# Loads of replicated tiles: four requests of 32 rows each, or one request of 128 rows, in a convolution-plus-scan kernel on one core

## The chip, the core and the metric

The kernel runs on one NeuronCore of one Trainium2 chip. The metric is the device time of one execution in microseconds (us). Three runs of the kernel before took 9806.04, 9808.63 and 9807.86 us; the median is 9807.86 us.

## What is computed

The input is 8 images of 256 channels and 48 x 48 = 2304 positions ("tokens"), float32. There are two layers, and each adds its result to its input after a group normalization (32 groups of 8 channels).

Layer 0 compares every token with every other and averages the features of the 16 nearest:

```python
feat_pos = tokens @ W.T + bias            # 256 features, 256 position channels
pos = pos / max(norm(pos), 1e-12)
sim = einsum('bnc,bmc->bnm', pos, pos)    # 2304 x 2304 per image
topksim, topkid = top_k(sim, 16)
out = einsum('bnk,bnkc->bnc', softmax(topksim), feat[topkid])
```

Layer 1 is a selective scan, two blocks deep (DEPTH = 2). With 512 inner channels (d) and 16 states (s) it is, for each token t in order,

```python
dA = exp(dt_t[:, :, None] * A)                                  # A is (512, 16)
h  = h * dA + dt_t[:, :, None] * B_t[:, None, :] * x_t[:, :, None]
y  = einsum('bds,bs->bd', h, C_t)
```

with a layer norm, an input projection, a causal convolution of 4 taps, SiLU and softplus before it, and a gate and an output projection behind it.

## The kernel before

**Units and steps.** Layer 1 is cut into chunks of T = 384 tokens, so 6 chunks for each of 8 images and 2 blocks: 96 units. A unit has 16 steps (STEPS = 512 / G with G = 32 channels) and each step has two parts, so a unit has 32 parts (HOOKS). In a step the 128 partitions hold 32 channels times J = 4 groups of states, and each partition carries Q = 4 states of 384 tokens. The step therefore needs its 32 rows of step sizes (`dt`) and of dt times x (`dtx`) four times, once in each quarter of the partitions, and the unit needs each row of B and of C in the 32 partitions of its group. These replicated tiles are `dtr`, `dtxr` and `BC`. They are made by writing `dt`, `dtx` and B, C to HBM (`times_x` L798, `split` L771) and reading them back (`load_rep` L615, `load_bc` L628). Each of the three kinds has three buffers.

**A step on the engines.** GpSimd (POOL) multiplies B by dtx (`make_bx`, L853), two steps ahead. ScalarE (ACT) makes the decays exp(dt A) into PSUM, two for each part (`decay`, L877). VectorE (DVE) runs the scan of a part, 770 elements (`run_scan`, L892). The product with C is then made by one of two engines: the strings SHARE say for each part of a unit whether POOL ("G", `pool_part`, L920) or DVE ("V", L894) does it. A step with "GG" is one POOL instruction of 1536 elements, a step with one "G" is one of 768. SHARE has three strings: the first for the nine units of an image that have the top-k beside them, the second for the other three, the third for the last image. TensorE (PE) sums the states (`sum_states`, L938).

**Order.** The order on each engine is the order in which the program names the instructions. The loop over parts at the end calls `carry`, `decay`, `make_bx`, `pool_part`, then the entries of a timetable for this part that stand before the scan (`between`), the scan, and the entries behind it (`behind`). An entry such as `(-8, load_rep, "dtx", 0)` puts that call 8 parts before its unit's first. Units with no top-k beside them use `between_spare` and `behind_spare`. All loads and stores of this phase are DMA requests in the queue of SyncE (SP), in that order; a request that waits for a semaphore holds what is behind it in this queue.

**Layer 0 beside it.** The first image's layer 0 runs alone; that of image n+1 runs beside the scan of image n (`Ahead.go`), with a table of its own (`within`) for each block of 128 tokens. `finish` (L535) adds a block's result, transposed in PSUM, to x, with the features' bias, and takes statistics for the next group normalization. `group_stats` (L187) combines them to a scale and a shift per channel.

**PSUM.** There are 8 banks. In the scan phase two decay tiles take 4, the tag "mm" takes 3 for all other products, and "po", the average of a block (`weigh`, L508), has one. When layer 0 runs alone, "mm" has 5 and "po" 2.

Of the kernel before, what the change touches and what calls it, by code (L numbers as in the profile page):

```python
# [15 lines left out]
P = 128  # L16
# [9 lines left out]
def tile_conv_preact(  # L26
# [45 lines left out]


    SHARE = (
        "GGVGGGVVGGGGGGVGGGVVGGGVGGGGGGVG",
        "GGGGVGVVGVVVGVGVGGGGVGVGGVVVGVGV",
        "VGVGVGVGVGVGGGVGGGVVVGVVGGVVGGVG",
    )
    assert N % T == 0 and N % P == 0 and T % P == 0 and NS % (J * HQ) == 0

# [106 lines left out]
    def group_stats(st, found, mm0, name):  # L187
# [69 lines left out]

    def layer0(b, left, pool, ps0, alone):
        def mm0(w, name):
            return ps0.tile([P, 512], F32, tag="mm", name=name, bufs=5 if alone else 3)[:, :w]  # L260

        more = 2 if alone else 1
        depth = 2 if alone else 1
# [271 lines left out]
        def finish(t):  # L535
            row = blocks[t]
            xr = row["xr"]

            for cb in range(CB):
                nc.vector.scalar_tensor_tensor(  # L540
                    xr[:, cb, :], row["pr"][:, cb * P : (cb + 1) * P], b_feat[:, cb : cb + 1],
                    xr[:, cb, :], ALU.add, ALU.add,
                )
                nc.vector.bn_stats(st1[:, cb, t, :], xr[:, cb, :])
            nc.sync.dma_start(x1[:, t * P : (t + 1) * P].rearrange("(k p) t -> p k t", p=P), xr)
            row.clear()
# [22 lines left out]
                f(t, *args)  # L569
            yield  # L570
        found = []
        yield from group_stats(st1, found, mm0, f"b{b}")
        left.update(x1=x1, rstd=found[0], shift=found[1])

    lefts = [{} for _ in range(B)]
# [29 lines left out]
        return banks[m % 2][:, 511 - T : 513 + T]  # L605

    def mm(w, name):
        return ps.tile([P, 512], F32, tag="mm", name=name, bufs=3)[:, :w]

# [5 lines left out]
    def load_rep(unit, what, ik):  # L615
# [345 lines left out]
    def leave(unit, cb):  # L961
# [22 lines left out]
        (10, load_rep, "dtx", 9), (21, load_rep, "dtx", 14), (11, gate, 0), (-29, spread_root),  # L984
        (0, times_x, 3), (-19, load_in, 5), (33, load_out), (8, load_rep, "dtx", 8), (-22, load_in, 0),
        (21, load_rep, "dt", 13), (-20, tap, 0), (-10, step_size, 1), (9, copy_z, 2), (-18, in_proj, 2),
        (2, load_rep, "dtx", 5), (10, sum_states, 0), (13, load_rep, "dt", 9), (29, gate, 2), (9, silu_z),
        (7, load_rep, "dt", 6), (19, load_rep, "dt", 12), (-6, load_rep, "dtx", 1), (-14, load_in, 7),
        (-30, root), (9, load_rep, "dt", 7), (4, load_d, 1), (-24, load_in, 3), (17, load_rep, "dt", 11),
        (14, load_rep, "dtx", 11), (-13, x_proj), (-17, load_in, 6), (-3, load_d, 0), (4, load_rep, "dtx", 6),  # L990
        (-4, load_rep, "dtx", 2), (-42, load_v),
    ]
    behind = [
        (-12, split), (-3, load_rep, "dt", 1), (3, in_proj, 4), (-10, step_size, 0), (-3, load_rep, "dt", 0),
        (-8, load_rep, "dtx", 0), (-15, tap, 3), (-1, load_rep, "dt", 2), (-28, scale),
        (16, load_rep, "dtx", 12), (11, load_rep, "dt", 8), (8, in_proj, 6), (17, sum_states, 1),
        (-14, silu_x), (25, load_rep, "dt", 15), (-37, affine), (1, times_x, 2), (7, copy_z, 0),
        (10, load_rep, "dtx", 10), (-17, tap, 2), (-10, softplus), (-16, in_proj, 3), (3, load_rep, "dt", 4),
        (-29, load_in, 2), (6, in_proj, 7), (35, gate, 3), (-2, load_rep, "dtx", 3), (8, copy_z, 1),
        (40, leave, 1), (22, load_rep, "dtx", 15), (-8, load_in, 4), (29, load_d, 3), (-37, mean),  # L1000
        (-19, taps, 0), (-19, in_proj, 1), (-10, load_bc, 0), (33, sum_states, 3), (-30, root_end),
        (-9, times_x, 0), (-20, load_in, 1),
    ]
    between_spare = [
        (-34, center), (24, sum_states, 2), (-34, variance), (-21, in_proj, 0), (38, out_proj, 0),
        (-15, taps, 2), (-14, taps, 3), (-35, square), (39, leave, 0), (20, load_rep, "dt", 14),
        (5, load_rep, "dt", 5), (-4, load_bc, 1), (38, out_proj, 1), (17, load_d, 2), (-17, tap, 1),
        (18, load_rep, "dtx", 13), (-8, times_x, 1), (19, gate, 1), (-22, normal), (9, load_rep, "dtx", 8),
        (1, load_rep, "dt", 3), (0, load_rep, "dtx", 4), (14, load_rep, "dt", 10), (6, load_rep, "dtx", 7),
        (10, load_rep, "dtx", 9), (-18, taps, 0), (12, load_rep, "dtx", 10), (20, load_rep, "dtx", 14),  # L1010
        (11, gate, 0), (-1, times_x, 2), (-22, spread_root), (-19, load_in, 5), (33, load_out),
        (-22, load_in, 0), (21, load_rep, "dt", 13), (-20, tap, 0), (-10, step_size, 1), (9, copy_z, 2),
        (-18, in_proj, 2), (2, load_rep, "dtx", 5), (10, sum_states, 0), (13, load_rep, "dt", 9),
        (29, gate, 2), (9, silu_z), (7, load_rep, "dt", 6), (19, load_rep, "dt", 12), (-6, load_rep, "dtx", 1),
        (-14, load_in, 7), (37, gate, 3), (-31, root), (9, load_rep, "dt", 7), (5, load_d, 1),
        (-24, load_in, 3), (17, load_rep, "dt", 11), (14, load_rep, "dtx", 11), (-13, x_proj),
        (-17, load_in, 6), (-3, load_d, 0), (4, load_rep, "dtx", 6), (-4, load_rep, "dtx", 2), (-42, load_v),
    ]
# [114 lines left out]
```

## Time and profile before

| | us |
|---|---|
| median of three runs | 9807.86 |
| the profiled execution | 9813.77 |
| its span, first to last instruction | 9812.0 |
| VectorE busy | 8904.6 (91%) |
| GpSimd busy | 9023.9 (92%) |
| TensorE busy | 7958.7 (81%) |
| ScalarE busy | 7304.4 (74%) |
| DMA queue of SP, share of 16 engines | 47.7% |

The profiled execution took 1.8 us more than its span. All durations of instructions below are from it. Busy times are averages over a span whose first 450 us, layer 0 of the first image, look different from the rest; so the shares are to be read by stage. The page's DMA lists give requests by what they write and read ("dtxr<-dtx_d"), their number, the size of one and the median time from issue to landing. The DMA share is the mean over 16 DMA engines: a share of 0.49 says nothing on how evenly the work lies on them.

### The profile page before, as it was taken

To read this page: it belongs to the slowest core of one execution; us is meant where nothing else is said; L and a number is where in the kernel's file an instruction comes from. 1 tells how busy PE (TensorE), PEld (TensorE's weight loads), DVE (VectorE), ACT (ScalarE), POOL (GpSimd) and SP (SyncE) were. 2 spreads that over 40 slices of the span, in tenths; PEclk is the share of its full clock that TensorE was granted. 3 is DMA by queue.
4 is the path that set the end of the run, shared out by engine and by line. 5 is a ranking of instruction groups with operands and counts; after the bars stand their busy time and mean duration, and the time that the engine had idled before them with its cause. 6 is when DMAs were issued, how large, how long until landed. Compare 5 with 4: busy or idle time off the path is not lost.

```text
span 9812.0 us, 133959 instructions
## 1 busy us (share of the span) xinstructions
PE 7958.7 (81%) x36761; PEld 4336.7 (44%) x36761; DVE 8904.6 (91%) x7864; ACT 7304.4 (74%) x15938; POOL 9023.9 (92%) x3971
## 2 busy tenths in 40 slices
PE   8888887888878887788877888778887788866665
PEld 6644443444434444444434445344443444422222
DVE  5599998999989999899988999899998999989898
ACT  4577877777777777777777787777786778767776
POOL 1199998999989999899999999999998999999999
PEclk9989998999989998899988999889998999977777
DMA  1244455545454445444454445544545454545554
GB/s 35 58 124 132 126 139 139 135 123 140 127 147 126 134 131 144 132 129 132 132 144 131 132 129 135 141 134 124 137 130 150 121 137 125 140 134 138 144 142 122
DMA packets 1241872, 1269.02 MB, mean 129 GB/s; under 512 B 266496, under 2 KB 1214208, under 8 KB 1241120
## 3 DMA queue, kind: packets, MB, share of 16 engines
q1 hardware_dynamic: 1240576, 1260.46, 47.7%
q8 instruction: 293, 4.80, 0.2%
q14 instruction: 459, 3.76, 0.1%
q10 hardware_dynamic: 544, 0.00, 0.0%
HBM read 1046.58 MB, written 212.86 MB: 128 GB/s over the span
## 4 chain that ended last, share of the span: by engine, by line
DVE 33%; ACT 24%; DMA 11%; PE 11%; SPq 10%; issue 7%; POOL 4%; ACTq 0%; DVEq 0%; POOLq 0%
DVE bx L892 11%; ACT da L877 10%; SPq L625 8%; DVE da L892 8%; DVE xc L751 5%; DMA dtr<-dt_d 4%; DVE bx L894 3%; DMA BC<-bc_d 3%; DVE top L464 2%; DVE left L467 2%; POOL bx L920 2%; PE po L514 2%; POOL bx L853 2%; DMA dtxr<-dtx_d 2%; ACT rest L486 1%
## 5 line engine op out<-in xcount | busy, mean ns | idle before, releaser
L853 POOL TENSOR_TENSOR bx<-BC,dtxr 128x1536 f32<-128x1536 f32 x1536 | 5296.3, 3454 | 144.5 <-PE y L938 72.8
L877 ACT ACTIVATE da<-dtr,A_sb 128x385 f32<-128x385 f32 x6144 | 3588.1, 584 | 868.6 <-DVE bx L892 375.1
L892 DVE TENSOR_TENSOR_SCAN bx<-da,bx 128x770 f32<-128x770 f32 x2073 | 3578.1, 1747 | 263.6 <-ACT da L877 232.4
L920 POOL TENSOR_TENSOR bx<-bx,BC 128x1536 f32<-128x1536 f32 (+1 forms) x1311 | 3353.6, 2558 | 70.5 <-DVE bx L892 66.0
L892 DVE TENSOR_TENSOR_SCAN da<-da,bx 128x770 f32<-128x770 f32 x999 | 1752.0, 1754 | 123.7 <-ACT da L877 81.2
L651 PE MATMUL pe<-vn,inw 128*128 128x384 f32 (+1 forms) x3072 | 1214.7, 526 | 329.6 <-issue 50.9
L514 PE MATMUL po<-feat,aT 128*128 128x256 f32 x5184 | 1352.3, 410 | 12.8 <-ACT aT L503 5.7
L938 PE MATMUL y<-bx,sel 128*32 128x384 f32 x12288 | 1266.0, 536 | 109.9 <-POOL bx L920 103.1
L443 PE MATMUL psim<-pos 128*128 128x512 f32 x2520 | 1215.2, 612 | 154.3 <-DVE xr L540 70.1
L514 PEld LDWEIGHTS po<-feat,aT 128*128 128x128 f32 x5184 | 1022.4, 203 | 343.1 <-issue 107.2
L894 DVE TENSOR_TENSOR bx<-da,BC 128x768 f32<-128x768 f32 x999 | 957.2, 958 | 34.4
L651 PEld LDWEIGHTS pe<-vn,inw 128*128 128x128 f32 x3072 | 566.9, 199 | 845.8 <-issue 206.2
L938 PEld LDWEIGHTS y<-bx,sel 128*32 128x32 f32 x12288 | 395.5, 118 | 961.5 <-issue 692.7
L443 PEld LDWEIGHTS psim<-pos 128*128 128x128 f32 x2520 | 478.0, 205 | 724.2 <-issue 375.5
L751 DVE SCALAR_TENSOR_TENSOR xc<-pe,cw,xc 128x384 f32<-128x384 f32 x1152 | 696.4, 611 | 43.4 <-ACT xc L743 16.3
L781 PE MATMUL pd<-dbl,dtp_sb 16*128 16x384 f32 x768 | 441.4, 689 | 336.5 <-ACT dt L790 189.9
L503 ACT ACTIVATE aT<-pt 128x512 f32<-128x512 f32 (+1 forms) x720 | 387.5, 548 | 419.8 <-PE pt L495 417.8
L956 PE MATMUL pw<-z,ow 128*128 128x384 f32 x1536 | 557.0, 509 | 112.8 <-ACT aT L503 52.4
L494 PE MATMUL pt<-ident,sim 128*128 128x128 f32 x2592 | 541.2, 290 | 18.5 <-ACT aT L503 13.6
L935 PE MATMUL y<-xc,dmat 128*128 128x384 f32 x768 | 398.3, 606 | 171.7 <-ACT h_st L930 58.5
L908 ACT COPY h_st<-da 128x2 f32<-128x2 f32 x808 | 128.6, 159 | 542.2 <-DVE bx L894 537.8
L495 PE MATMUL pt<-minus,rest 128*128 128x128 bf16 x2592 | 492.9, 224 | 5.9 <-ACT rest L486 5.8
(155 smaller groups left out, 9966.9 us busy)
## 6 DMA issues: line engine op xcount, KB each, us to landing
dtxr<-dtx_d SPq DMA_DIRECT2D x6144, 48.0 KB, 1.9
dtr<-dt_d SPq DMA_DIRECT2D x6144, 48.0 KB, 1.9
BC<-bc_d SPq DMA_DIRECT2D x768, 192.0 KB, 3.9
inw<-in_in_wT_dram SPq DMA_DIRECT2D x768, 128.0 KB, 2.3
dtx_d<-dtx SPq DMA_DIRECT2D x384, 192.0 KB, 2.3
dt_d<-dt SPq DMA_DIRECT2D x384, 192.0 KB, 2.3
ow<-in_out_wT_dram SPq DMA_DIRECT2D x96, 512.0 KB, 4.0
dmat<-diag SPq DMA_DIRECT2D x384, 64.0 KB, 2.2
```

The source lines that it names most:

```text
L443: nc.tensor.matmul(pm, pos[:, k, t * P : (t + 1) * P], pos[:, k, c0 : c0 + w], start=(k == 0), stop=(k == CB - 1),)
L514: nc.tensor.matmul(row["po"], aT[:, m % PT, :], feat[:, m, :], start=(m == 0), stop=(m == NB - 1))
L625: nc.sync.dma_start(rows[j * G : (j + 1) * G], src[:, i0, :])
L651: nc.tensor.matmul(pe, w[:, k], unit["vn"][:, k, lo:], start=(k == 0), stop=(k == CB - 1))
L751: nc.vector.scalar_tensor_tensor(unit["xc"][e], unit["pe"][e][:, k : k + T], cw[:, unit["d"], e, k : k + 1], unit["xc"][e], ALU.mult, ALU.add,
L853: nc.gpsimd.tensor_tensor(bx[:, :, 1:], unit["BC"][0], unit["dtxr"][i].unsqueeze(1).to_broadcast([P, Q, T]), ALU.mult,)
L877: nc.scalar.activation(da[:, s * (1 + T) : (s + 1) * (1 + T)], unit["dtr"][i], AF.Exp, scale=A_sb[:, unit["d"], i, p * HQ + s : p * HQ + s ...
L892: nc.vector.tensor_tensor_scan(h, da, g, 0.0, ALU.mult, ALU.add)
L894: nc.vector.tensor_tensor(bx[:, :, 0:T], da.rearrange("p (q t) -> p q t", q=HQ)[:, :, 1:], unit["BC"][1][:, qs], ALU.mult,)
L920: nc.gpsimd.tensor_tensor(g[:, :, 0:T], g[:, :, 1:], unit["BC"][1][:, qs], ALU.mult)
L938: nc.tensor.matmul(y[j * G : (j + 1) * G, :], sel, unit["bx"][k * J + j][:, q, 0:T], start=False, stop=True, skip_group_check=True,)
L956: nc.tensor.matmul(pw, unit["ow"][:, k, cb * P : (cb + 1) * P], unit["z"][k], start=(k == 0), stop=(k == DB - 1),)
```

## The change

There are five edits.

1. `load_rep` and `load_bc`: a tile is loaded by one request. Its source is read four times over (dt, dtx), or each of four pieces 32 times over (B, C). The number of these requests falls from 6144 + 6144 + 768 to 1536 + 1536 + 192; the bytes written are the same.
2. PSUM: the tile "po" is taken from the tag "mm", which has 4 banks beside the scan (7 when layer 0 runs alone).
3. SHARE: some parts change from POOL to DVE and the other way.
4. The features' bias: `finish` adds a block in one instruction of 256 elements, without bias. The bias is added to the group's means before they are combined (`group_stats`, `more`), enters the shift, and is added once more to the final result (`leave`).
5. The timetables: a few entries move by up to 4 parts (the loads of dt 15 and dtx 14, `affine`, `center`, `scale`, `spread_root`, `times_x` 2), and some lines stand in another order.

The core of the diff:

```diff
-        "GGVGGGVVGGGGGGVGGGVVGGGVGGGGGGVG",
-        "GGGGVGVVGVVVGVGVGGGGVGVGGVVVGVGV",
-        "VGVGVGVGVGVGGGVGGGVVVGVVGGVVGGVG",
+        "GGVGGGVVGGGGGGVGGGVVGGGVGGGGGVVG",
+        "GVGGVGVVGVVVGVGVGGGGVGVVGVGVGVGV",
+        "VGVGVGVGVGVVGGGVGGGVVGVVGVVGGGVG",
...
+        if more is not None:
+            nc.vector.tensor_add(mv[:, :, 0], mv[:, :, 0], more)
...
-        nc.gpsimd.tensor_mul(shift, mean, rstd)
-        nc.gpsimd.tensor_scalar(shift, shift, -1.0, None, ALU.mult)
+        if more is None:
+            nc.gpsimd.tensor_scalar(shift, mean, -1.0, None, ALU.mult)
+        else:
+            nc.gpsimd.tensor_sub(shift, more, mean)
+        nc.gpsimd.tensor_mul(shift, shift, rstd)
...
-            return ps0.tile([P, 512], F32, tag="mm", name=name, bufs=5 if alone else 3)[:, :w]
+            return ps0.tile([P, 512], F32, tag="mm", name=name, bufs=7 if alone else 4)[:, :w]
...
-                row["po"] = ps0.tile([P, 512], F32, tag="po", name=f"po_{b}_{t}", bufs=more)[:, :C]
+                row["po"] = mm0(C, f"po_{b}_{t}")
...
+            nc.vector.tensor_add(xr, xr, row["pr"].rearrange("p (k t) -> p k t", k=CB))
             for cb in range(CB):
-                nc.vector.scalar_tensor_tensor(
-                    xr[:, cb, :], row["pr"][:, cb * P : (cb + 1) * P], b_feat[:, cb : cb + 1],
-                    xr[:, cb, :], ALU.add, ALU.add,
-                )
                 nc.vector.bn_stats(st1[:, cb, t, :], xr[:, cb, :])
...
         src = unit[f"{what}_d"][k].rearrange("(i g) t -> g i t", g=G)
-        for j in range(J):
-            nc.sync.dma_start(rows[j * G : (j + 1) * G], src[:, i0, :])
+        nc.sync.dma_start(rows, src[:, i0, :].partition_broadcast(J))
...
-        for j in range(J):
-            r0 = i * NS + j * Q
-            nc.sync.dma_start(
-                t[j * G : (j + 1) * G].rearrange("p q t -> p (q t)"),
-                unit["bc_d"][r0 : r0 + Q, :].rearrange("q t -> (q t)").partition_broadcast(G),
-            )
+        src = unit["bc_d"][i * NS : (i + 1) * NS, :].rearrange("(j q) t -> j (q t)", j=J)
+        nc.sync.dma_start(
+            t.rearrange("p q t -> p (q t)"), src.unsqueeze(1).to_broadcast([J, G, Q * T])
+        )
...
-            nc.vector.tensor_add(res[:, cb, :], res[:, cb, :], unit["pw"][cb])
+            nc.vector.scalar_tensor_tensor(
+                res[:, cb, :], unit["pw"][cb], b_feat[:, cb : cb + 1], res[:, cb, :], ALU.add, ALU.add
+            )
```

Of the timetables, `(25, load_rep, "dt", 15)` in `behind` becomes `(28, load_rep, "dt", 15)` and `(21, load_rep, "dtx", 14)` becomes `(19, load_rep, "dtx", 14)`; in the spare tables `(20, load_rep, "dtx", 14)` becomes `(17, load_rep, "dtx", 14)`, `(-34, center)` becomes `(-36, center)`, `(-22, spread_root)` becomes `(-26, spread_root)` and `(-21, scale)` becomes `(-25, scale)`.

More of the change, by code (lines that the diff above doesn't have):

```diff
@@ L185, in rsqrt_end, with group_stats @@
         eng.scalar_tensor_tensor(r, var, 1.5, r, ALU.subtract, ALU.mult)
-    def group_stats(st, found, mm0, name):
+    def group_stats(st, found, mm0, name, more=None):
         mv = small.tile([P, CB, 2], F32, tag="gn_mv", name=f"mv_{name}")
@@ L571, in layer0 @@
         found = []
-        yield from group_stats(st1, found, mm0, f"b{b}")
+        yield from group_stats(st1, found, mm0, f"b{b}", b_feat)
         left.update(x1=x1, rstd=found[0], shift=found[1])
@@ L607, in mm @@
     def mm(w, name):
-        return ps.tile([P, 512], F32, tag="mm", name=name, bufs=3)[:, :w]
+        return ps.tile([P, 512], F32, tag="mm", name=name, bufs=4)[:, :w]
     def load_rep(unit, what, ik):
@@ L983, in tile_conv_preact @@
         (1, load_rep, "dt", 3), (0, load_rep, "dtx", 4), (15, load_rep, "dt", 10), (6, load_rep, "dtx", 7),
[L984 to L991, printed above, removed]
+        (10, load_rep, "dtx", 9), (11, gate, 0), (-29, spread_root), (0, times_x, 3), (-19, load_in, 5),
+        (33, load_out), (8, load_rep, "dtx", 8), (-22, load_in, 0), (21, load_rep, "dt", 13), (-20, tap, 0),
+        (-10, step_size, 1), (9, copy_z, 2), (-18, in_proj, 2), (2, load_rep, "dtx", 5), (10, sum_states, 0),
+        (13, load_rep, "dt", 9), (29, gate, 2), (9, silu_z), (7, load_rep, "dt", 6), (19, load_rep, "dt", 12),
+        (-6, load_rep, "dtx", 1), (-14, load_in, 7), (-30, root), (9, load_rep, "dt", 7), (4, load_d, 1),
+        (-24, load_in, 3), (17, load_rep, "dt", 11), (14, load_rep, "dtx", 11), (-13, x_proj),
+        (-17, load_in, 6), (-3, load_d, 0), (4, load_rep, "dtx", 6), (-4, load_rep, "dtx", 2), (-42, load_v),
     ]
@@ L996, in tile_conv_preact @@
         (16, load_rep, "dtx", 12), (11, load_rep, "dt", 8), (8, in_proj, 6), (17, sum_states, 1),
[L997 to L1000, printed above, removed]
@@ L1001, in tile_conv_preact @@
-        (-19, taps, 0), (-19, in_proj, 1), (-10, load_bc, 0), (33, sum_states, 3), (-30, root_end),
-        (-9, times_x, 0), (-20, load_in, 1),
+        (-14, silu_x), (28, load_rep, "dt", 15), (-39, affine), (2, times_x, 2), (7, copy_z, 0),
+        (19, load_rep, "dtx", 14), (10, load_rep, "dtx", 10), (-17, tap, 2), (-10, softplus),
+        (-16, in_proj, 3), (3, load_rep, "dt", 4), (-29, load_in, 2), (6, in_proj, 7), (35, gate, 3),
+        (-2, load_rep, "dtx", 3), (8, copy_z, 1), (40, leave, 1), (22, load_rep, "dtx", 15), (-8, load_in, 4),
@@ L1003, in tile_conv_preact @@
+        (29, load_d, 3), (-37, mean), (-19, taps, 0), (-19, in_proj, 1), (-10, load_bc, 0),
+        (33, sum_states, 3), (-30, root_end), (-9, times_x, 0), (-20, load_in, 1),
     ]
     between_spare = [
-        (-34, center), (24, sum_states, 2), (-34, variance), (-21, in_proj, 0), (38, out_proj, 0),
-        (-15, taps, 2), (-14, taps, 3), (-35, square), (39, leave, 0), (20, load_rep, "dt", 14),
-        (5, load_rep, "dt", 5), (-4, load_bc, 1), (38, out_proj, 1), (17, load_d, 2), (-17, tap, 1),
@@ L1008, in tile_conv_preact @@
[L1008 to L1016, printed above, removed]
+        (24, sum_states, 2), (-34, variance), (-21, in_proj, 0), (38, out_proj, 0), (-15, taps, 2),
@@ new lines, in tile_conv_preact @@
+        (-14, taps, 3), (-35, square), (39, leave, 0), (20, load_rep, "dt", 14), (5, load_rep, "dt", 5),
+        (-4, load_bc, 1), (38, out_proj, 1), (17, load_d, 2), (-17, tap, 1), (18, load_rep, "dtx", 13),
+        (-8, times_x, 1), (19, gate, 1), (-22, normal), (9, load_rep, "dtx", 8), (1, load_rep, "dt", 3),
+        (0, load_rep, "dtx", 4), (14, load_rep, "dt", 10), (6, load_rep, "dtx", 7), (10, load_rep, "dtx", 9),
+        (-18, taps, 0), (12, load_rep, "dtx", 10), (17, load_rep, "dtx", 14), (11, gate, 0), (-1, times_x, 2),
@@ new lines, in tile_conv_preact @@
+        (-19, load_in, 5), (33, load_out), (-22, load_in, 0), (21, load_rep, "dt", 13), (-20, tap, 0),
+        (-10, step_size, 1), (9, copy_z, 2), (-18, in_proj, 2), (2, load_rep, "dtx", 5), (10, sum_states, 0),
+        (13, load_rep, "dt", 9), (29, gate, 2), (9, silu_z), (7, load_rep, "dt", 6), (19, load_rep, "dt", 12),
+        (-6, load_rep, "dtx", 1), (-14, load_in, 7), (37, gate, 3), (-31, root), (9, load_rep, "dt", 7),
+        (5, load_d, 1), (-24, load_in, 3), (17, load_rep, "dt", 11), (14, load_rep, "dtx", 11), (-13, x_proj),
@@ L1017, in tile_conv_preact @@
         (-17, load_in, 6), (-3, load_d, 0), (4, load_rep, "dtx", 6), (-4, load_rep, "dtx", 2), (-42, load_v),
+        (-36, center), (-26, spread_root),
     ]
@@ L1020, in tile_conv_preact @@
         (-12, split), (-3, load_rep, "dt", 1), (4, in_proj, 4), (-10, step_size, 0), (-5, load_rep, "dt", 0),
-        (-8, times_x, 3), (-8, load_rep, "dtx", 0), (-15, tap, 3), (-1, load_rep, "dt", 2), (-21, scale),
+        (-8, times_x, 3), (-8, load_rep, "dtx", 0), (-15, tap, 3), (-1, load_rep, "dt", 2),
         (16, load_rep, "dtx", 12), (11, load_rep, "dt", 8), (8, in_proj, 6), (17, sum_states, 1),
@@ L1026, in tile_conv_preact @@
         (-16, load_in, 4), (29, load_d, 3), (-38, mean), (-21, in_proj, 1), (-12, load_bc, 0),
-        (33, sum_states, 3), (-31, root_end), (-9, times_x, 0), (-25, load_in, 1),
+        (33, sum_states, 3), (-31, root_end), (-9, times_x, 0), (-25, load_in, 1), (-25, scale),
     ]
```

## The prediction

> **What bounds the kernel now.** I read the busy shares and the chain first, then busy time by stage, then the costly groups by form, and last the DMA lists, because the change is mostly one of DMA requests.
>
> ```profile
> PE 7958.7 (81%) x36761; PEld 4336.7 (44%) x36761; DVE 8904.6 (91%) x7864; ACT 7304.4 (74%) x15938; POOL 9023.9 (92%) x3971
> DVE 33%; ACT 24%; DMA 11%; PE 11%; SPq 10%; issue 7%; POOL 4%; ACTq 0%; DVEq 0%; POOLq 0%
> ```
>
> ```profile
> 453.00:8424.00 7971.00, 6655.50 (x30907) 3633.03 (x30906) 7418.31 (x6530) 6113.08 (x13366) 7644.69 (x3278) 0.91 0.49 133
> 8424.00:9812.00 1388.00, 904.33 (x3760) 401.51 (x3758) 1246.95 (x1067) 970.69 (x2112) 1333.48 (x552) 0.79 0.51 136
> ```
>
> The second fence gives PE, PE's loads, DVE, ACT and POOL busy in the scan phase. POOL is at 96% in both stretches, DVE at 93% and 90%: there is at most 4% to win without lightening POOL. The chain changes hands often, and 10% of it is SP's queue issuing. The timeline gives the pace: the store of B and C, once in a unit, is issued at 438.55 (unit 0), 8725.82 (unit 84) and 9691.27 us (unit 95), so a unit takes 98.7 us with layer 0 beside it and 87.8 us in the last image.
>
> ```profile
> L853 POOL TENSOR_TENSOR bx<-BC,dtxr 128x1536 f32<-128x1536 f32 x1536 | 5296.3, 3454 | 144.5 <-PE y L938 72.8 <-DMA dtxr<-dtx_d 37.6 <-ACT da L877 23.6
> L877 ACT ACTIVATE da<-dtr,A_sb 128x385 f32<-128x385 f32 x6144 | 3588.1, 584 | 868.6 <-DVE bx L892 375.1 <-DMA dtr<-dt_d 255.3 <-DVE bx L894 94.4
> L920 POOL TENSOR_TENSOR bx<-bx,BC 128x1536 f32<-128x1536 f32 x762 | 2427.1, 3185 | 60.4 <-DVE bx L892 56.0 <-DVE den L479 1.0 <-DMA dtxr<-dtx_d 0.3
> L894 DVE TENSOR_TENSOR bx<-da,BC 128x768 f32<-128x768 f32 x999 | 957.2, 958 | 34.4
> L920 POOL TENSOR_TENSOR bx<-bx,BC 128x768 f32<-128x768 f32 x549 | 926.5, 1688 | 10.1 <-DVE bx L892 10.1
> ```
>
> The replicated loads now cost waits of 255.3 us on ACT and 37.6 us on POOL, in 9812.
>
> ```profile
> DMA packets 1241872, 1269.02 MB, mean 129 GB/s; under 512 B 266496, under 2 KB 1214208, under 8 KB 1241120
> q1 hardware_dynamic: 1240576, 1260.46, 47.7%
> ...
> dtxr<-dtx_d SPq DMA_DIRECT2D x6144, 48.0 KB, 1.9
> dtr<-dt_d SPq DMA_DIRECT2D x6144, 48.0 KB, 1.9
> BC<-bc_d SPq DMA_DIRECT2D x768, 192.0 KB, 3.9
> ```
>
> The DMA engines look half idle. That holds only if a request lies on all 16.
>
> ```profile
> 8.00:10.00 2.00, 0.00 (x0) 0.00 (x0) 1.98 (x7) 0.00 (x0) 0.00 (x0) 1.00 1.07 398
> ```
>
> This is the one full stretch (8 to 10 us, queued loads, rows of 1536 B mostly): share 1.07 at 398 GB/s, so one engine moves 24.9 GB/s.
>
> **The requests, row first.** By the trace every request runs on 16 engines: SP issues 15,918, times 16 is 254,688, and the page has 266,496 packets under 512 B, which fits one completion packet per engine and request, with some small rows. If that stays so, a tile of 4 x 49,152 = 196,608 B lands about like dt_d's store of the same size (2.3 us), its last quarter earlier than now (four issues at a median of 419 ns, 1.7 us, against one).
>
> [...]
>
> **What four engines cost.** A dt or dtx tile is 49,152 B per engine, at 24.9 GB/s 1.97 us; a B or C tile 196,608 B, 7.90 us. A unit has 32 and 2: 63.0 + 15.8 = 78.8 us. The rest: all tiles together are 3072 x 0.1966 + 192 x 0.7864 = 755 MB of 1260.46; of the other 505 some 23 lie before 453 us, so 482 / 96 = 5.0 MB a unit over 16 engines, 12.6 us on each. Sum 91.4 us of a unit's 98.7, 93%; in the last image layer 0's 0.83 MB a unit fall away, 89.4 against 87.8, 102%. So the four are just full on average, and the order decides:
> - Parts -10 to 2 of a unit (12 of 32, 37.0 us) carry both B and C (15.8), twelve dt/dtx tiles (23.6), six stores (6 x 0.49), `load_v` and small ones (1.6): 44 us, 7 behind.
> - `load_rep dtx 0` waits in SP's queue for the store of dtx 0, which stands behind B's 7.9 us on the four engines. SP issues nothing meanwhile, and they run dry for an issue and a landing, some 2.5 us.
> - The tiles have three buffers, so a load goes out at most about two steps (12.3 us) before it is needed; that hides a part of the 9.5. I take 6 us late per unit with layer 0 (0 if hidden, 12 if nothing is) and 10 in the last image.
>
> 84 x 6 + 12 x 10 = 624 us. Who waits: ACT's decays for `dtr`, then DVE's scan, and POOL's L853 for `dtxr`.
>
> SP's own issuing falls from 13,056 of these requests to 3264; at 0.42 us, 4.1 ms of queue time go. It is worth only what arrives earlier: at most the 293 us of waits above, and nothing when the engines behind are full. A request of the new form may take from 0.34 us (dtx_d's store of 128 rows) to 1.7 us (the four it replaces); either hides behind the transfer of 1.97.
>
> **SHARE.** Units by string: 63, 21, 12. G+G steps fall from 762 to 666, steps with one G rise from 549 to 657, V parts from 999 to 1083. POOL: -96 x 3.185 + 108 x 1.688 = -123 us. DVE: +84 x 0.958 = +80 us. ACT's carries (159 to 180 ns): +13 us.
>
> **Bias.** `finish`: 288 x 339 ns go. 144 additions of 256 elements from PSUM come: between 128x384 (L973, 537) and 128x768 (L685, 945) the slope is 1.06 ns an element, so 401 ns; 57.7 - 97.6 = -40 us on DVE. L973 becomes the form of L751 (611): 96 x 74 ns = +7. `more`: 8 x 161 ns (L185) = +1 us, on the path only for image 0's statistics. POOL has two small instructions either way.
>
> Sum: POOL -123, DVE +48. POOL is the fullest, DVE has 3% more room, so I count -30 us (from -123, POOL alone the bound, to +60, if DVE's scans are late).
>
> **Banks.** "po" holds a bank for 5 of every 16 parts and leaves it to others else. PSUM's waits for banks now (PE's L443 for ACT's copy and DVE's `finish`, 58 + 70) bound the gain by -130; a product waiting behind a held "po" could cost the same. I take 0: PE is 84% busy and 11% of the chain.
>
> **Timetables.** Nothing is added. Moved loads (dt 15, dtx 14) pass a few entries of SP's queue and still stand before their use; the moved DVE pieces (`center` 945, `scale` 931 ns) and the small rest stay under POOL's 96%. 0, -20 to +20; dt 15 now stands one part before its decay, and is late first if its engines are.
>
> **Sum.** 9813.8 (execution) - 30 + 624 = 10,408; the median stands 6 us below the profiled execution (0.06%): about 10,400.
>
> **The rivals.**
> 1. *Four engines, hidden.* 91.4 is under 98.7, and if the buffers smooth the bursts only the last image pays (1.6 us a unit) against -30: 9750 to 9850. Against it: the bursts at a unit's start, and dtx 0's wait.
> 2. *Sixteen engines; ends faster.* [...] Then the last quarter of each tile lands 1.3 us earlier. I give a third of the 293 us of waits, -98, and -30: 9680. [...] For it: every request seen has 16.
> 3. *Four engines, below the full rate.* On the page's bill q1 spent 47.7% of 16 x 9812 us on 1260 MB, 16.8 GB/s per busy engine, waiting included. At 20 GB/s a unit needs 114 us: 453 + 96 x 114 + 50 = 11,450; at 16.8, 135 us and 13,500. Against it: 398 GB/s in a full queue.
>
> **How the numbers follow.** Main case 0.60 (9900 to 11,100); rival 1 0.14; rival 2 0.12; rival 3 0.14. About 0.2% (20 us) is what a measurement of this kernel can tell. Faster: rival 2's 0.10 and 0.04 of rival 1, 0.14. Within 0.2%: 0.05, mostly rival 1. Slower: 0.81. The range leaves out rival 2's and the slow end of rival 3: 9750 to 11,700. Low and high sizes of the small edits (-150 to +100) lie inside it.
>
> **What would show it.** Right: the page lists `dtr` and `dtxr` x1536 at 192.0 KB with 5 us or more to landing, BC x192 above 9; packets under 512 B fall by about 196,000 (13,056 x 16 less 3264 x 4); ACT's wait for `dtr` and POOL's for `dtxr` are several hundred us each, POOL's share falls below 90%. Wrong: tiles landing near 2.5 us, only some 157,000 small packets fewer, POOL still at 95%. L920 at 666 and 657 and L894 at 1083 would show SHARE; a large wait of PE for the bank of "po" would overturn the banks' zero.

## The result, and the profile after

The changed kernel takes 11,621.28 us (median of 4 runs, 11,605.08 to 11,631.93) where the kernel before takes 9806.95 (9803.53 to 9808.63): 1.1849 times as long (95% interval 1.1829 to 1.187), 1814 us more. The prediction was 10,400, or 594 more. The sign came out as predicted, and so did the number of engines as the cause; the size is three times as large.

The page of the kernel after: span, busy shares, DMA totals, the chain by engine.

```profile
span 11602.9 us, 120531 instructions
PE 8153.8 (70%) x36761; PEld 4579.6 (39%) x36761; DVE 8988.2 (77%) x7812; ACT 7279.5 (63%) x16018; POOL 8907.3 (77%) x3983
...
DMA packets 1045928, 1267.38 MB, mean 109 GB/s; under 512 B 70657, under 2 KB 1018369, under 8 KB 1045281
q1 hardware_dynamic: 1044736, 1259.67, 34.4%
...
DMA 35%; DVE 22%; ACT 18%; PE 11%; issue 6%; POOL 6%; SPq 2%; ACTq 0%; POOLq 0%; DVEq 0%
```

Three things are to be seen. First, POOL and DVE have about the work that they had: POOL is busy 117 us less and DVE 84 us more (the sum had -123 and +48), and both have fallen to 77% of the span. Time was added in which they wait. Second, the chain now runs through DMA for 35% instead of 11%, while the queue's share of the 16 engines fell from 47.7% to 34.4%: the transfers became the bound while the mean said that the DMA engines had become idler. Third, the small packets tell on how many engines a request lies. They fell by 266,496 - 70,657 = 195,839. If each of the 13,056 old requests leaves 16 small packets and each of the 3264 new ones 4, the fall is 208,896 - 13,056 = 195,840; at 16 it would have been 156,672. So the new requests run on four engines: alone, in e7_alone (below), they keep 0.26 to 0.27 of the 16 busy.

The groups of POOL's product and ACT's decay (count, busy, mean ns, idle before and its main releaser), and the largest waits for DMA from the view of waits (us in total, times, longest):

```profile
L852 POOL TENSOR_TENSOR bx<-BC,dtxr 128x1536 f32<-128x1536 f32 x1536 | 5289.8, 3448 | 1389.4 <-DMA dtxr<-dtx_d 1131.3
L876 ACT ACTIVATE da<-dtr,A_sb 128x385 f32<-128x385 f32 x6144 | 3591.3, 585 | 2761.1 <-DMA dtr<-dt_d 2014.7
```

```profile
ACT da L876 <- DMA dtr<-dt_d: 2014.7, 323, 19.7
POOL bx L852 <- DMA dtxr<-dtx_d: 1131.3, 268, 11.1
SPq L626 <- DMA dtx_d<-dtx: 579.5, 70, 10.2
```

One product and one decay cost what they did (3448 against 3454 ns, 585 against 584); their waits for replicated tiles went from 37.6 to 1131.3 us and from 255.3 to 2014.7. 323 waits in 96 units, up to 19.7 us long, are few and large: some 3.4 a unit. The third line is SP waiting before a load of dtx until the rows have been stored, 70 times and up to 10.2 us.

**Where in a unit the time goes.** The busy times by stretch (us, PE, PEld, DVE, ACT, POOL, granted clock, DMA share, GB/s), for one unit with layer 0 beside it, cut at the end of its start. First the kernel before, whose unit stores B and C at 2997.11, then the kernel after, which stores them at 4059.46:

```profile
3000.00:3029.00 29.00, 24.70 (x121) 15.68 (x121) 28.86 (x24) 21.31 (x46) 28.57 (x11) 0.86 0.67 173
3029.00:3094.00 65.00, 58.28 (x286) 30.88 (x284) 62.07 (x59) 53.37 (x122) 65.00 (x25) 0.98 0.42 115
```

```profile
4059.00:4109.00 50.00, 25.56 (x112) 15.04 (x112) 31.70 (x24) 24.94 (x55) 34.27 (x13) 0.76 0.32 102
4109.00:4176.00 67.00, 61.23 (x298) 34.41 (x298) 63.68 (x59) 53.60 (x125) 62.84 (x22) 0.95 0.36 114
```

The first stretch moves the same 5.0 MB in both (29 us at 173 GB/s, 50 us at 102) and holds much the same work (DVE x24 in both). It takes 50 us instead of 29. The second takes 67 instead of 65, at the same 114 to 115 GB/s. So nearly all of the loss lies where B, C and the first tiles of a unit are fetched. 102 GB/s is about what four engines alone give (99 to 105 in e7_alone, below), though the row says a DMA share of 0.32.

SP's queue in that stretch (start, duration, line, request) shows why. First two requests of the unit of before, then the unit of after:

```profile
3007.32 0.37 SPq L804 DMA_DIRECT2D dtx_d<-dtx  x1
...
3010.29 3.44 SPq L625 DMA_DIRECT2D dtxr<-dtx_d  x4
```

```profile
4059.46 0.34 SPq L775 DMA_DIRECT2D bc_d<-dbl  x1
...
4061.64 0.51 SPq L633 DMA_DIRECT2D BC<-bc_d  x1
...
4065.75 0.34 SPq L803 DMA_DIRECT2D dtx_d<-dtx  x1
...
4072.18 0.38 SPq L803 DMA_DIRECT2D dt_d<-dt  x1
4081.85 0.54 SPq L626 DMA_DIRECT2D dtxr<-dtx_d  x1
...
4083.60 0.52 SPq L633 DMA_DIRECT2D BC<-bc_d  x1
...
4084.79 1.13 SPq L626 DMA_DIRECT2D dtr<-dt_d  x1
4086.01 8.35 SPq L528 DMA_DIRECT2D xr<-in_x_dram  x1
4094.45 3.76 SPq L737 DMA_DIRECT2D dmat<-diag  x2
4098.31 2.43 SPq L626 DMA_DIRECT2D dtr<-dt_d  x2
```

The store of dtx 0 is issued at 4065.75, the load that reads it only at 4081.85: 16.1 us later, where the unit of before needed 3.0 (3007.32 to 3010.29). B's request of 4061.64 lies ahead of the store on the four engines: of the 16 completions that the trace has of the store, twelve come from 4067.46 to 4067.64 and the other four from 4079.16 to 4081.79, behind B's four (4076.73 to 4079.30). SP issues nothing from 4072.6 to 4081.85. For most of this time the four engines still work off what they have, and they are dry for about 2 us at its end (rows as above):

```profile
4074.00:4080.00 6.00, 5.67 (x32) 4.24 (x30) 6.00 (x5) 1.83 (x5) 4.32 (x2) 1.00 0.26 91
4082.00:4084.00 2.00, 0.75 (x3) 0.68 (x4) 1.31 (x1) 2.00 (x5) 0.00 (x0) 1.00 0.04 13
```

Then dtx 0, dtx 1, C, dtx 2 and a tile of dt (4084.79) follow, one after another, and two more of dt. The tile of 4084.79 is dt 15 of the unit that is ending: the requests for dt, counted in the program's order, are 16 a unit. ACT's decays in the same stretch (idle before, and for what, in brackets), for steps 14 and 15 of the ending unit and step 0 of the new one, and in the last line for step 0 in the unit of before:

```profile
4081.39 1.20 ACT L876 ACTIVATE da<-dtr,A_sb 128x385 f32<-128x385 f32 x2 [5.10 <-DMA dtr<-dt_d]
4104.25 1.20 ACT L876 ACTIVATE da<-dtr,A_sb 128x385 f32<-128x385 f32 x2 [17.44 <-DMA dtr<-dt_d]
...
4109.51 1.21 ACT L876 ACTIVATE da<-dtr,A_sb 128x385 f32<-128x385 f32 x2
```

```profile
3029.05 1.21 ACT L877 ACTIVATE da<-dtr,A_sb 128x385 f32<-128x385 f32 x2 [2.28 <-DMA dtr<-dt_d]
```

From the store of B and C to the first decay of the unit's step 0, 50.05 us pass (4059.46 to 4109.51); before, 31.94 (2997.11 to 3029.05). The difference is 18.1 us. The periods of units, from one store of B and C to the next, say the same: with layer 0 beside it (10,266.18 - 444.32) / 84 = 116.9 us against 98.7, and in the last image (11,461.08 - 10,266.18) / 11 = 108.6 against 87.8. That is 18.2 and 20.8 us a unit, 84 x 18.2 + 11 x 20.8 = 1758 of the 1791 us between the two profiled executions.

Which tiles are late can be counted too (ACT's decays in the program's order, four a step). Of its 2014.7 us of waits for dt, 1174.1 stand before step 15 of the ending unit, 405.8 before its steps 13 and 14, and 372.9 before steps 0 to 4 of the new one. So the tile waited for most is an old one. The rows of dt 15 are stored at part 0 of its unit (`times_x` 3), and its buffer, that of dt 12, is free from 4070.0 in the unit shown. But in SP's queue its load stands behind the wait for the store of dtx 0, and on the four engines behind C.

### The profile page after: what moved, and what is told of

The parts are those of the page before. It is cut to its first block, busy times and chain, and to the rows that moved or that the text cites. A ratio compares the mean times of both kernels' runs of the same rounds, so it can differ in the third digit from the quotient of the medians.

```text
span 11602.9 us, 120531 instructions
## 1 busy us (share of the span) xinstructions
PE 8153.8 (70%) x36761; PEld 4579.6 (39%) x36761; DVE 8988.2 (77%) x7812; ACT 7279.5 (63%) x16018; POOL 8907.3 (77%) x3983
## 2 busy tenths in 40 slices
DMA packets 1045928, 1267.38 MB, mean 109 GB/s; under 512 B 70657, under 2 KB 1018369, under 8 KB 1045281
## 3 DMA queue, kind: packets, MB, share of 16 engines
q1 hardware_dynamic: 1044736, 1259.67, 34.4%
## 4 chain that ended last, share of the span: by engine, by line
DMA 35%; DVE 22%; ACT 18%; PE 11%; issue 6%; POOL 6%; SPq 2%; ACTq 0%; POOLq 0%; DVEq 0%
DMA dtr<-dt_d 24%; ACT da L876 8%; DMA dtxr<-dtx_d 7%; DVE bx L891 7%; DVE da L891 5%; DVE xc L750 4%; POOL bx L852 3%; PE psim L448 2%; ACT rest L491 2%; POOL bx L919 2%; PE y L937 2%; DVE top L469 2%; DVE left L472 2%; PE pe L650 2%; DMA inw<-in_in_wT_dram 2%
## 5 line engine op out<-in xcount | busy, mean ns | idle before, releaser
L852 POOL TENSOR_TENSOR bx<-BC,dtxr 128x1536 f32<-128x1536 f32 x1536 | 5289.8, 3448 | 1389.4 <-DMA dtxr<-dtx_d 1131.3
L876 ACT ACTIVATE da<-dtr,A_sb 128x385 f32<-128x385 f32 x6144 | 3591.3, 585 | 2761.1 <-DMA dtr<-dt_d 2014.7
L891 DVE TENSOR_TENSOR_SCAN bx<-da,bx 128x770 f32<-128x770 f32 x1989 | 3441.5, 1749 | 295.3 <-ACT da L876 253.3
L919 POOL TENSOR_TENSOR bx<-bx,BC 128x1536 f32<-128x1536 f32 (+1 forms) x1323 | 3225.6, 2438 | 415.4 <-DVE bx L891 410.4
L891 DVE TENSOR_TENSOR_SCAN da<-da,bx 128x770 f32<-128x770 f32 x1083 | 1903.9, 1758 | 1455.6 <-ACT da L876 1272.2
L519 PE MATMUL po<-feat,aT 128*128 128x256 f32 x5184 | 1445.7, 431 | 245.3 <-ACT aT L508 207.3
L519 PEld LDWEIGHTS po<-feat,aT 128*128 128x128 f32 x5184 | 1075.6, 215 | 626.0 <-ACT aT L508 289.8
L697 PE MATMUL lv<-ones_mean,lsq 128*128 128x1 f32 x1152 | 259.9, 353 | 1469.1 <-ACT lsq L691 1300.3
L893 DVE TENSOR_TENSOR bx<-da,BC 128x768 f32<-128x768 f32 x1083 | 1037.9, 958 | 136.1 <-DMA BC<-bc_d 99.5
L697 PEld LDWEIGHTS lv<-ones_mean,lsq 128*128 128x128 f32 x1152 | 251.7, 328 | 1548.2 <-ACT lsq L691 1376.5
L448 PEld LDWEIGHTS psim<-pos 128*128 128x128 f32 x2520 | 512.7, 216 | 649.3 <-issue 424.9
L800 POOL TENSOR_TENSOR dtx<-dt,xc 128x384 f32<-128x384 f32 x384 | 384.9, 1002 | 399.5 <-DMA dtx_d<-dtx 266.4
L508 ACT ACTIVATE aT<-pt 128x512 f32<-128x512 f32 (+1 forms) x720 | 387.6, 548 | 374.8 <-PE pt L500 372.9
```

The lines of the kernel that those rows point to most:

```text
L448: nc.tensor.matmul(pm, pos[:, k, t * P : (t + 1) * P], pos[:, k, c0 : c0 + w], start=(k == 0), stop=(k == CB - 1),)
L519: nc.tensor.matmul(row["po"], aT[:, m % PT, :], feat[:, m, :], start=(m == 0), stop=(m == NB - 1))
L852: nc.gpsimd.tensor_tensor(bx[:, :, 1:], unit["BC"][0], unit["dtxr"][i].unsqueeze(1).to_broadcast([P, Q, T]), ALU.mult,)
L876: nc.scalar.activation(da[:, s * (1 + T) : (s + 1) * (1 + T)], unit["dtr"][i], AF.Exp, scale=A_sb[:, unit["d"], i, p * HQ + s : p * HQ + s ...
L891: nc.vector.tensor_tensor_scan(h, da, g, 0.0, ALU.mult, ALU.add)
L893: nc.vector.tensor_tensor(bx[:, :, 0:T], da.rearrange("p (q t) -> p q t", q=HQ)[:, :, 1:], unit["BC"][1][:, qs], ALU.mult,)
```

## The experiments

Each ratio is against runs of the kernel before that were made beside it (medians 9793.52, 9807.03 and 9794.85). The first theory was four engines per request, with a shortage of DMA capacity in the unit's start; its rivals were a slower rate per engine, and edits other than the requests.

**e1_rest: the change without the requests.** Four requests a tile as before, the other four edits as in the change.

```diff
-        nc.sync.dma_start(rows, src[:, i0, :].partition_broadcast(J))
+        for j in range(J):
+            nc.sync.dma_start(rows[j * G : (j + 1) * G], src[:, i0, :])
```

`load_bc` likewise.

> The changed kernel with its replicated tiles loaded by four requests again; the other four edits stay. If the requests alone cost the 1800 us: 9740 to 9830 us (9810 less some 30, plus or minus 50), dtr and dtxr again x6144 at 1.9 us to landing. If banks, SHARE or timetables carry a part of the loss: 9950 us or more.

9679.77 us, ratio 0.9884 (0.9869 to 0.9899): 114 us faster than before, outside what was expected. The whole loss comes with the requests.

**e2_requests: the requests alone.** The kernel before with the changed `load_rep` and `load_bc`.

```diff
-        for j in range(J):
-            nc.sync.dma_start(rows[j * G : (j + 1) * G], src[:, i0, :])
+        nc.sync.dma_start(rows, src[:, i0, :].partition_broadcast(J))
```

> The kernel before with only the replicated loads changed to one request. If the requests carry it all: 11,650 us, within 100, and 70,700 packets under 512 B as in the changed kernel. If the other edits carry a part: below 11,400 us.

11,582.68 us, ratio 1.1827 (1.1804 to 1.1851). That is all of the loss, with 70,656 packets under 512 B. Here dt 15 is loaded at part 25, ahead of C, and not at 28 as in the change, and ACT's waits for dt (1847.5 us) lie elsewhere: 893.6 before step 0, 128.9 before step 15. So the place of dt 15 decides which decay waits, and not how much is lost. The two intervals, this one and the change's, overlap: beside slow loads the other edits, worth 114 us in e1_rest, show nothing.

**e3_spread: one request on 16 engines.** Partition p holds channel p // 4 and group of states p % 4, so the copies stand inside the 32 rows and the outermost size is 32. `sel` and A's layout follow.

```diff
-        nc.sync.dma_start(rows, src[:, i0, :].partition_broadcast(J))
+        nc.sync.dma_start(rows, src[:, i0, :].unsqueeze(1).to_broadcast([G, J, T]))
...
-        nc.sync.dma_start(
-            t.rearrange("p q t -> p (q t)"), src.unsqueeze(1).to_broadcast([J, G, Q * T])
-        )
+        nc.sync.dma_start(t.rearrange("p q t -> p (q t)"), src.partition_broadcast(G))
```

> [...] If the number of engines is the cause: 9600 to 9780 us, dtr and dtxr x1536 landing in 2 to 3 us, about 110,000 packets under 512 B, ACT's wait for dtr under 300 us. If a single large request is what costs (its issue, its later landing): over 11,000 us.

9662.51 us (9661.02 to 9663.05), ratio 0.9866 (0.985 to 0.9883): faster than before and than the change. The page of e3_spread, its packets and its requests (the last figure is us from issue to landing), and then its decay in the view of groups:

```profile
DMA packets 1084999, 1267.54 MB, mean 131 GB/s; under 512 B 109728, under 2 KB 1057440, under 8 KB 1084352
...
dtr<-dt_d SPq DMA_DIRECT2D x1536, 192.0 KB, 2.7
BC<-bc_d SPq DMA_DIRECT2D x192, 768.0 KB, 5.4
```

```profile
L872 ACT ACTIVATE da<-dtr,A_sb 128x385 f32<-128x385 f32 x6144 | 3591.6, 585 | 956.3 <-DVE bx L887 706.2 <-DVE bx L889 107.7 <-DMA dtr<-dt_d 6.5
```

The number of requests and of bytes is the change's. Only the order of two dimensions differs, and ACT's wait for dt is 6.5 us instead of 2014.7. The small packets fell by 156,768, close to the 156,672 of 16 engines. So the loss is not in the size of a request or in its repeated reading, but in the number of engines.

**e7_alone: the loads by themselves.** No computation: the output is zeros, and five series of loads go into eight buffers in turn: 256 dt tiles and 64 B tiles in the change's form, 256 dt tiles whose four copies come from four places in DRAM, then 512 dt and 128 B tiles in e3_spread's form.

```diff
+    for n in range(256):
+        nc.sync.dma_start(small[n % 8], rows[:, n % 4, :].partition_broadcast(J))
...
+    for n in range(256):
+        nc.sync.dma_start(small[n % 8], far[:, :, n % 4, :])
...
+    for n in range(512):
+        nc.sync.dma_start(small[n % 8], rows[:, n % 4, :].unsqueeze(1).to_broadcast([G, J, T]))
```

> Nothing of the computation; it writes zeros to the output and then only loads tiles, eight buffers in turn, in five stretches: 256 dt tiles by four copies outermost; 64 B tiles by four pieces outermost; 256 dt-like tiles from four different blocks of rows; 512 dt tiles with 32 rows outermost; 128 B tiles with 32 outermost. Theory 1 (an engine with a full queue moves about 20 GB/s in this shape, not 24.9): 2.3 to 2.6 us a dt tile and 9.3 to 10 a B tile in the first two stretches. Theory 2 (24.9 GB/s when fed; the rest was lost in waits): 1.95 to 2.05 and 7.8 to 8.1 us. If it is four engines reading one row at a time that slows them, the third stretch is faster than the first by over 10%. The last two: about 0.55 us a dt tile (one issue each) and 2.0 to 2.6 a B tile.

SP's queue (start, duration of a series), and three stretches (us, DVE, POOL, granted clock, DMA share, GB/s) from the first three series:

```profile
33.10 514.07 SPq L78 DMA_DIRECT2D dtr<-dt_d  x256
547.22 460.92 SPq L82 DMA_DIRECT2D BC<-bc_d  x64
1008.17 523.65 SPq L87 DMA_DIRECT2D dtr<-far_d  x256
1531.87 338.44 SPq L90 DMA_DIRECT2D dtr<-dt_d  x512
1870.35 232.23 SPq L94 DMA_DIRECT2D BC<-bc_d  x128
```

```profile
100.00:500.00 400.00, 0.00 (x0) 0.00 (x0) 1.00 0.27 100
650.00:1100.00 450.00, 0.17 (x1) 0.00 (x0) 1.00 0.26 105
1200.00:1250.00 50.00, 0.00 (x0) 0.00 (x0) 1.00 0.27 99
```

514.07 / 256 = 2.01 us for a dt tile on four engines (the sum had 1.97); the series begins while the stores of the zeros still run, and its later rate of 100 GB/s makes 1.97. For B 477.8 us until the last has landed, / 64 = 7.47 us (the sum had 7.90). A share of 0.27 at 100 GB/s is four of 16 engines full, at 25 GB/s each; up to eight requests are under way, so they all lie on the same four. Reading one row with four engines at once cost nothing: from four separate places a tile takes 1.98 us (507.5 us of waiting for 256), from one place 1.97 to 2.01. In e3_spread's form the same tiles take 338.44 / 512 = 0.66 us, where SP's issuing is the limit (a median of 602 ns each), and those of B and C 243.7 / 128 = 1.90 us until the last has landed. So the shape of the request did not slow an engine. In the kernel it is otherwise for B and C: their packets of 6144 bytes took 316 ns on average there, against 236 in the second series here (and 395 in the kernel before), which makes 10.1 us a tile (32 packets on each of four engines) for 7.5. What slows them was not tested.

**e4_bc and e5_dt: half of the requests each.** The kernel before, with only B and C (e4), or only dt and dtx (e5), in the new form.

```diff
-            nc.sync.dma_start(
-                t[j * G : (j + 1) * G].rearrange("p q t -> p (q t)"),
-                unit["bc_d"][r0 : r0 + Q, :].rearrange("q t -> (q t)").partition_broadcast(G),
-            )
...
+        nc.sync.dma_start(
+            t.rearrange("p q t -> p (q t)"), src.unsqueeze(1).to_broadcast([J, G, Q * T])
+        )
```

> The kernel before with one request for each B and C tile (four pieces outermost, so four engines), dt and dtx still by four requests on 16 engines. The four engines then have some 44 us of work in a unit of 98.7. If the loss is one of capacity: 9780 to 9850 us. If it is one of order at a unit's start (a B or C of 7.4 us on four engines stands ahead of the store that SP waits for, and of the first dt tile): 4 to 6 us a unit, 10,150 to 10,400.

> The kernel before with one request for each dt and dtx tile (four engines), B and C still by four requests on 16. The four engines have some 80 us of work a unit. Capacity or order without the long B and C: 9850 to 10,150 us. If the loss is a longer landing of each tile, paid step by step all through the unit: over 10,800. With the run before, if the two losses together are well under the 1790 us of both, the two kinds compound at the unit's start.

e4_bc: 10,999.38 us, ratio 1.1217 (1.1184 to 1.1249), +1192. e5_dt: 10,701.39, ratio 1.0913 (1.0881 to 1.0945), +894. Both cost far more than expected, so capacity summed over a unit does not decide alone. In e4_bc the four engines carry 2 x 7.47 us of B and C and a quarter of the work in the rest, 32 x 0.5 + 12.6: 44 us, or 50 with the 10.4 us that the packets of B and C took there. A unit takes 110. They are less than half full, and yet a unit takes 12 us more than before. What the two add alone, 2086, is more than they add together (1792 in e2_requests), as if they delayed the same stretch. The waits of e4_bc, of SP and of ACT (us in total, times, longest):

```profile
SPq L625 <- DMA BC<-bc_d: 1218.8, 128, 11.6
SPq L802 <- DMA BC<-bc_d: 424.5, 63, 8.4
ACT da L875 <- DMA dtr<-dt_d: 1337.2, 279, 16.1
```

SP's loads of dt and dtx (L625), and its stores (L802), wait for B or C to land, of which they need nothing. In the traces of before and of the change the queue's requests name eight completion semaphores in turn (100 to 104 and 106 to 108), and SP waits for a semaphore before it uses it again. So a request goes out only when the one eight before it has landed, and a slow one of B or C stops the queue. With four requests a tile, as in e4_bc, eight are just two tiles. That is how I read these waits; no run changed the number of semaphores. In the change eight requests are eight tiles, and these two waits of SP for B or C are 20.7 us in all. So e4_bc loses its time in another way than the change does: it shows that a unit can lose 12 us with the four engines half empty, not how the change loses 18.

**e6_two: two requests a tile.** The kernel before with two copies a request. What was expected takes two engines for such a request; four copies had run on four, and no run had shown two.

```diff
-        for j in range(J):
-            nc.sync.dma_start(rows[j * G : (j + 1) * G], src[:, i0, :])
+        for j in range(0, J, 2):
+            nc.sync.dma_start(rows[j * G : (j + 2) * G], src[:, i0, :].partition_broadcast(2))
```

> [...] A unit then needs 170 us of those two at 25 GB/s. Full rate when the queue is never empty: 16,800 to 18,000 us. If an engine moves only 20 GB/s beside the other traffic: about 20,800. [...]

18,214.04 us (one run), 1.86 times the kernel before and a little over what was expected. Fewer requests than before, but more than in the change, and far slower than either: the number of engines sets the time. The stretch of scans in e6_two:

```profile
470.00:18000.00 17530.00, 8564.40 (x34417) 4541.64 (x34419) 8676.47 (x7528) 7006.47 (x15362) 8900.99 (x3793) 0.71 0.21 71
```

A unit takes (18,212 - 453) / 96 = 185 us. Two engines at 24.9 GB/s need 32 x 3.95 + 2 x 15.8 + 12.6 = 170. Here, where they are really the bound, 92% of the time is full-rate transfer.

**e8_late_c and e11_late_b: the order in the unit's start.** In the change, C's load moved from part -4 to -1 (e8); B's from parts -10 and -12 to -8, behind the load of dtx 0 (e11).

```diff
-(5, load_rep, "dt", 5), (-4, load_bc, 1), (38, out_proj, 1),
+(5, load_rep, "dt", 5), (-1, load_bc, 1), (38, out_proj, 1),
```

```diff
-(-19, in_proj, 1), (-10, load_bc, 0),
+(-19, in_proj, 1), (-8, load_bc, 0),
```

> The changed kernel with one entry of the timetables moved: the load of C at part -1 in place of -4, behind the first two dt tiles of its unit. The same bytes on the same four engines. Order at the unit's start: the dt tile of step 0 lands some 7 us earlier; C, dt 2 and what follows come later, so that 2 to 7 us a unit are won: 10,950 to 11,430 us. Capacity: unchanged within 60 of 11,620.

> The changed kernel with the load of B moved from part -10 (-12 in the spare table) to -8, behind the stores of dt and dtx 0 and the load of dtx 0. The same bytes on the same four engines. If SP's wait for the store of dtx 0, which now stands behind B's 7.4 us, is a main term of the hole at a unit's start: dtx 0 lands some 8 us earlier and B later, and 5 to 8 us a unit are won, 10,850 to 11,140 us. If the four engines' amount of work at the unit's start is what counts, whatever its order: 11,560 to 11,680.

e8_late_c: 11,471.55 us, ratio 1.1698 (1.1664 to 1.1732). e11_late_b: 11,466.63, ratio 1.1707 (1.1686 to 1.1728). Each wins some 150 us, 1.6 us a unit, less than expected. Their waits moved and did not go. In e8_late_c ACT and POOL wait less, and DVE waits for C instead (805.4 us, in the change 99.5):

```profile
ACT da L876 <- DMA dtr<-dt_d: 1425.9, 438, 8.9
POOL bx L852 <- DMA dtxr<-dtx_d: 831.5, 259, 10.1
DVE bx L893 <- DMA BC<-bc_d: 805.4, 96, 16.6
```

In e11_late_b the wait on dtx 0's store is indeed short: issued at 4019.01, the load follows at 4025.93. But then B, C and the tiles follow on the four engines all the same, and ACT waits nearly as long (1848.7 us, 1470.2 of them before step 15). POOL's product and ACT's decay in the timeline of e11_late_b:

```profile
4040.89 3.42 POOL L852 TENSOR_TENSOR bx<-BC,dtxr 128x1536 f32<-128x1536 f32 x1 [9.31 <-DMA BC<-bc_d]
```

```profile
4054.97 1.20 ACT L876 ACTIVATE da<-dtr,A_sb 128x385 f32<-128x385 f32 x2 [18.14 <-DMA dtr<-dt_d]
```

So neither of these two entries alone is the cause: what is moved ahead no longer waits, and what is moved behind waits instead. At the rates of e7_alone B (7.5 us), C (7.5) and the first four or five tiles (2.0 each) make some 24 us one after another on four engines, where 16 would take about 6; both are estimates, and at 10.1 us each for B and C it is nearer 29. The data of B, C and the new unit's tiles exists only shortly before, and the ending unit's last tiles stand in the same queue.

**e9_share and e10_banks: where the 114 us of the other edits come from.** e1_rest with SHARE as before (e9), and with the banks as before (e10):

```diff
-        "GVGGVGVVGVVVGVGVGGGGVGVVGVGVGVGV",
+        "GGGGVGVVGVVVGVGVGGGGVGVGGVVVGVGV",
...
```

```diff
-            return ps0.tile([P, 512], F32, tag="mm", name=name, bufs=7 if alone else 4)[:, :w]
+            return ps0.tile([P, 512], F32, tag="mm", name=name, bufs=5 if alone else 3)[:, :w]
...
-                row["po"] = mm0(C, f"po_{b}_{t}")
+                row["po"] = ps0.tile([P, 512], F32, tag="po", name=f"po_{b}_{t}", bufs=more)[:, :C]
```

> The first experiment's kernel (four requests per tile, the other four edits) with SHARE of before. If the 114 us that it won against before come from POOL's 123 us less: 9780 to 9810 us. If they come from banks, bias and timetables: within 30 of 9680.

> The first experiment's kernel with the PSUM banks of before (three and one; five and two when layer 0 runs alone). If the four common banks carry a good part of the 114 us: 9730 to 9790 us. If they are worth nothing, as predicted: 9660 to 9700.

e9_share: 9746.21 us, ratio 0.995 (0.9938 to 0.9963), so the new SHARE is worth about 0.66%, 65 us, in that company. e10_banks: 9799.33, ratio 1.0001 (0.9992 to 1.001): without the banks the other three edits win nothing, so the banks are worth some 115 us there. 65 and 115 are more than 114 together: either the two need each other, or the bias and the timetables cost some time; no run separates this. PE's waits before the products of dt in e10_banks (first line) and e1_rest (second):

```profile
PE pd L783 <- ACT dt L792: 193.1, 96, 3.9
```

```profile
PE pd L783 <- ACT dbl L776: 132.9, 87, 4.4
```

In e10_banks PE waits 96 times, once a unit, until ACT has read dt out of its bank; with four common banks this wait falls to 17.4 us in all, and what is left is the wait for data.

**e3b_spread: the spread loads alone.** The kernel before with e3_spread's form of the two loads, `sel` and A.

```diff
-        for j in range(J):
-            nc.sync.dma_start(rows[j * G : (j + 1) * G], src[:, i0, :])
+        nc.sync.dma_start(rows, src[:, i0, :].unsqueeze(1).to_broadcast([G, J, T]))
```

> The kernel before with only the loads changed: one request per tile with 32 rows outermost (channel p // 4 on partition p), so on 16 engines. What one request instead of four is worth when the engines stay 16: by the difference of the third and first experiment some 17 us, so 9770 to 9800; if SP's issuing (10% of the chain before) was a bound, 9680 to 9740.

9765.18 us, ratio 0.997 (0.9958 to 0.9981). One request in place of four, with all 16 engines kept, is worth some 30 us. Its chain by engine:

```profile
DVE 51%; ACT 19%; PE 12%; issue 10%; POOL 5%; DMA 3%; SPq 0%; DVEq 0%; POOLq 0%; ACTq 0%
```

SP's queue had 10% of the chain before and has none here, DMA 3% instead of 11%. The time fell by 0.3%. I read this so: that share stood in for other work that ends at about the same time, and was not time to be won.

Not tried: more buffers for dt and dtx; dt 15 requested ahead of dtx 0; the bias and the timetables alone; another number of completion semaphores.

## Why the prediction was right or wrong

**Right: how many engines.** The sum counts four engines for a request of the new form, the same four for all tiles, where every request of before has 16. No run or trace showed either at that time; both were assumed. The runs showed both. The fall in small packets agrees within one packet with four engines. It agrees with two in e6_two (70,656 left, with twice as many requests as in the change), and nearly with 16 in e3_spread (156,768 against 156,672). That the four are always the same ones is seen in e7_alone (up to eight requests under way, a share of 0.27), and in the unit shown: the last four completions of the store of dtx 0 come behind B's four. Rival 2 (16 engines, 9680) is refuted by the change, and is what e3_spread makes of it: 9662.51 by another order of the same copies.

**Right: the price of a tile alone. Too low: the unit's sum.** 1.97 and 7.90 us were worked out from a stretch of 2 us at the start of the trace; alone, 1.97 to 2.01 and 7.47 were measured. But in the kernel a tile of B or C cost 10.1 us. Counted from the packets' times in steps of 0.25 us, about four or more DMA engines are at work at once in 89% of the time after the first 500 us (in e7_alone's first two series in all of it). That is an estimate of 104 of a unit's 116.9 us, where the sum had 91.4. So the four were nearly full, and their work took longer than summed.

**Wrong: "I take 6 us late per unit with layer 0 ... and 10 in the last image".** Measured: 18.2 and 20.8. This term is the error: 624 us in the sum, 1758 in the trace. It had three parts:
- The dry time of 2.5 us was about right (some 2 us in the unit shown).
- The excess of work in the unit's start, 7 us, was too small: B and C took 10.1 us each instead of 7.90, 4.4 us more a unit.
- The buffers were to hide 3.5 of the 9.5 us, and nothing shows that they hid any. A free buffer helps only a load that the queue lets out. In the unit shown the buffer of dt 15 is free at 4070.0 and its rows have long been stored, but it is requested at 4084.79 and lands behind C.

The 9.5 with nothing hidden and the 4.4 make 13.9 of the 18.2 us, an estimate from these numbers; the other 4 stay open. The sum weighed the load of the stretch against its length. The path through the stretch was at hand too: some 24 us of B, C and tiles on four engines, where 16 take 6, is 18 more. That this agrees with 18.2 is in part luck, for B and C were slower than it takes them.

**Rival 1 (hidden, 9750 to 9850)** fell because its argument was the average, 91.4 under 98.7, which was itself too low. **Rival 3 (below the full rate)** came nearest, 11,450. As a property of the request's shape it is refuted by e7_alone, at 25 GB/s an engine. For B and C in the kernel it holds: 6144 bytes in 316 ns are 19 GB/s.

**Small edits.** The sum had -30. Alone they are worth -114 (e1_rest). Without the banks, taken at 0 with a bound of -130, nothing of it is left (e10_banks); without the new SHARE, under half is left. Beside the slow loads they are worth nothing that the intervals of e2_requests and of the change can tell apart, so -30 was not what failed. The counts are as read from the tables: POOL -117 us for -123, DVE +84 for +48.

**The marks.** The waits (2014.7 and 1131.3), POOL's share (77%), the packets and the x1536 all came as told, and so did dt 15, which "is late first if its engines are". The time from issue to landing can't be read: the page of the kernel after gives none for these requests.

## What to carry to other kernels

For a load that repeats its source, try the rows outermost and the repetition inside them: 32 rows outermost ran on 16 engines here, four copies outermost on four. Only the order of the partitions had to change for it (1.1849 became 0.9866). To see whether the DMA engines are full, compare with the engines that a request uses, not with the mean share: 0.32 was nearly full here. And for a loop, price a slower transfer along the queue: what the first user of new data waits for, and which older tiles stand behind that in the same queue. An average says nothing of this, and a free buffer is of no use to a load that the queue holds back.

## What was not expected of the hardware

- Issuing itself held SP while earlier requests were still under way: in the unit shown, a request for `xr` held SP for 8.35 us and two for `dmat` for 3.76, against 0.34 for a store; the longest of the new requests held it for 10.7 us, at a median of 537 ns.
- A request on all 16 engines waited behind one on four: the store of dtx 0, issued 4.1 us after B's request, let its reader go 16.1 us later (before, 3.0), with twelve of its 16 completions within 1.9 us and the last four 13.4 to 16.0 us after its issue.
- Four engines reading the same row lost nothing (1.97 to 2.01 us, against 1.98 from four places).
- The same packets of B and C took 316 ns in the kernel and 236 alone, on the same four engines.
- PE's 36,761 products took 195 us more (8153.8 against 7958.7) at a mean granted clock of 0.82 against 0.895: in the unit's start, where PE is half idle, the clock's row shows 0.76, in the rest 0.95.
